# A graph layer with experts: the test for stray edges put off, the count matrix cleared by transfers, gathered chunks prepared first

## The chip, the cores and the metric

The kernel runs as one program on one core of a Trainium2 chip. The metric is the device time of one execution in microseconds (us); smaller is better. The kernel before has a median of 2081.84 us over three runs (2081.11 to 2084.28).

The engines have these names in the profile: PE (matrix products) with PEld (its loads of weights), DVE (elementwise work, reductions), ACT (elementwise work with functions), POOL (here: constants, clears, and the issue of indirect transfers) and SP (issues of plain transfers; its queue is SPq). ACT and POOL issue transfers too.

## The reference

There are 6,250 nodes with 256 features and 100,000 directed edges, sorted by destination. The destination of an edge is 6250 u^2 for a uniform u, so low nodes have many more edges than high ones; the sources are uniform.

```python
def _L0_gnn_ref(x, edge_index, weight, bias):
    src, dst = (edge_index[0], edge_index[1])
    summed = jax.ops.segment_sum(x[src], dst, num_segments=n)
    deg = jax.ops.segment_sum(ones, dst, num_segments=n)
    agg = summed / jnp.maximum(deg, 1.0)[:, None]
    out = jnp.concatenate([x, agg], axis=-1) @ weight
    return out / jnp.linalg.norm(out, axis=-1, keepdims=True) + bias
...
x = _layernorm(x + _L0_gnn_ref(x, edge_index, L0_gnn_weight, L0_gnn_bias), axis=-1)
...
deg_out = jnp.clip(jax.ops.segment_sum(ones, src, num_segments=n), 1.0)
deg_in = jnp.clip(jax.ops.segment_sum(ones, dst, num_segments=n), 1.0)
h = feats * jax.lax.rsqrt(deg_out)[:, None]
m = jax.ops.segment_sum(h[src], dst, num_segments=n) * jax.lax.rsqrt(deg_in)[:, None]
x = (m @ W_gc + b_gc) + (feats @ W_res + b_res)
y = x + _moe_ff(x, Wg, bg, w1, b1, w2, b2)   # top 2 of 64 experts
```

After that come a normalisation over the nodes, a residual and a second layer norm. The change concerns the two segment sums (each node's sum over the rows of its neighbours) and the degrees; the rest is the same in both kernels.

## The kernel before, in words

**Edges.** The edges are cut into 782 chunks of 128, in order of destination. For both layers the sums are made in two ways. The first 216 chunks hold all edges into the first 512 nodes and are *counted*: products of one-hot matrices on PE (L741, from selections that DVE builds at L727) give how often each source occurs for each destination, and DVE adds the counts into `adj`, a matrix of 49 x 816 bf16 on each of 128 partitions (L733). Later `adj` times the rows of all nodes is an ordinary dense product (L416). It has to be zero before the first count. The other 566 chunks are *gathered*: POOL issues one indirect transfer per chunk (L379, `gather_rows`), which brings the 128 source rows into `rows`, and a one-hot selection matrix `oh` sums them by destination on PE (L649 for rows of `x` in f32, L667 for rows in three bf16 parts). Neighbouring chunks make a group; the group's sum is turned (L386) and added into `acc` (L393), which is 2 x NACC f32 on each partition and has to be zero before that.

The first 64 of the gathered chunks take f32 rows of `x` itself, through seven buffers. The others take rows of `x3_rows`, three bf16 parts of `x`, which the kernel writes to DRAM first: SP loads five parts of `x` into `xt`, ACT casts them (L700), and SP writes `x3_rows`. They have nine buffers. For f32 rows `oh` is built by ACT for even chunks (L594 and L595, from `iota_row` and the column of `rel` for the chunk) and by DVE for odd ones (L592). The second layer gathers 518 chunks from `h_rows` in the same way (L1135).

**Preparation, L263 to L371.** ACT issues loads of the bias and of the weights `w0`. `nothing` is 512 zeros. `acc`'s first half is cleared by DVE (L266), the second half by ACT (L274); five eighths of `adj` by POOL (L270), the rest by ACT (L274). Then, on DVE in this order: the cast of `dst` to f32 (`dst_f`, L289); with `upmost` two products on PE that give the first destination of each chunk, copied to `first`; `base`, the first destination of a chunk's group, by a copy for each run of groups with the same size; `gbase`, the same by groups, and `base_i`, its integers; `wlo` and `whi`, the two halves of the window's node numbers; `rel`, an edge's destination less its base, for counted and for gathered chunks. Then the **test for stray edges**: an edge whose `rel` lies outside its window, or a group that lies before the dense part, sets `bad`; PE adds it over the partitions (`pbad`), and the result `any_bad` is 0 or 1. From it come `extra` (the trip counts 782 and 49, or 0), `sound` (1 or 0), and an offset OUTSIDE that is added to all of `rel`, so that with a stray edge no fast path counts anything. Then `hi` and `lo` of the sources, and `near`, the bf16 copy of `rel` for the gathered chunks.

**A way for any order.** Loops whose trip counts are read from `extra` (L437 in `any_order`, over all chunks, and L895 and L1202, over all 49 tiles of nodes) compute the layers edge by edge where the test has found a stray edge. With these inputs the trip counts are 0 and no body runs. The trip counts are loaded into registers at step 12 of the first stage (L878).

**Order.** In the first stage the order on PE, DVE, ACT and SP is written out by hand, and the engines' programs keep it: one step for each gathered chunk, and `work(i)` does what else is due at step i. A `Track` spreads its items evenly from step `begin` to step `end`: casts and writes of `x3_rows` until step 44 (X_END), counting until step 304 (A_END), the counts by source (`hist`, the out-degrees, through PSUM `ph`) until 350 (H_END), the dense product until 485 (D_END). `out_degrees` at H_END + 2 turns the counts by source into the factors of the second layer. The first layer's tiles follow as their nodes become complete (`first_layer`), with writes of `x1_rows` and `h_rows`. POOL is not part of this order: it issues the gathers one after the other, each as soon as its buffer is free.

The engines meet at the end of the first stage (the loops L437 and L895 with no trips, the first gather from `h_rows`) and at the end of the second stage (the loops of the second `any_order` and L1202). Then come the gating, the sorting of rows to the experts, and the experts.

Of the kernel before, what the change touches and what calls it, by code (L numbers as in the profile page):

```python
# [19 lines left out]
P = 128  # L20
# [125 lines left out]
def gnn_moe_kernel(  # L146
# [75 lines left out]
    sound = keep.tile([P, 1], F32, name="sound")  # L222

    with ExitStack() as gctx:
# [41 lines left out]
        nc.vector.memset(acc[:, 0, :], 0.0)  # L266
        flat = adj.rearrange("p t d -> p (t d)").bitcast(F32)
        total = NT * (DENSE + MORE) // 2
        by_pool = total * 5 // 8
        nc.gpsimd.memset(flat[:, :by_pool], 0.0)  # L270
        for v, a, b in ((acc[:, 1, :], 0, NACC), (flat, by_pool, total)):
            for i in range(a, b, 512):
                n = min(512, b - i)
                nc.scalar.copy(v[:, i : i + n], nothing[:, :n])  # L274
        with tc.tile_pool(name="pl", bufs=1) as pl, tc.tile_pool(name="pps", bufs=1, space=PSUM) as pps:
# [13 lines left out]
            nc.vector.tensor_copy(dst_f, dst_i)  # L289
            upmost = pl.tile([P, P], F32, name="upmost")  # L290
            nc.vector.tensor_scalar(upmost, ones, iota_p, None, op0=OP.is_gt)
            pfirst = pps.tile([P, 2, 512], F32, name="pfirst")
# [15 lines left out]
            for i, c0, col, g, n in runs:  # L308
                gv = first[:, c0 : c0 + n * g].rearrange("p (n g) -> p n g", g=g)
                nc.vector.tensor_copy(base[:, col : col + n * g].rearrange("p (n g) -> p n g", g=g),  # L310
                                      gv[:, :, 0:1].to_broadcast([P, n, g]))
# [3 lines left out]
            gbase = pl.tile([P, ng], F32, name="gbase")  # L315
            for i, c0, col, g, n in runs:
                nc.vector.tensor_copy(gbase[:, i : i + n],
                                      base[:, col : col + n * g].rearrange("p (n g) -> p g n", g=g)[:, 0, :])
            nc.vector.tensor_copy(base_i, gbase[0:1, :])
# [3 lines left out]
            wdst = pl.tile([P, ng], I32, name="wdst")  # L323
            nc.vector.tensor_scalar(wdst, gbase, iota_p, None, op0=OP.add)
            wtmp = pl.tile([P, ng], I32, name="wtmp")
            nc.vector.tensor_single_scalar(wtmp, wdst, 7, op=OP.arith_shift_right)
            nc.vector.tensor_copy(whi, wtmp)
            nc.vector.tensor_single_scalar(wtmp, wdst, P - 1, op=OP.bitwise_and)
            nc.vector.tensor_copy(wlo, wtmp)
            nc.vector.tensor_sub(rel[:, :DCH], dst_f[:, :DCH], base[:, :DCH])  # L330
            nc.vector.tensor_sub(rel[:, DCH:], dst_f[:, GCH:], base[:, DCH:])
# [13 lines left out]
            pbad = pps.tile([P, 2], F32, name="pbad")  # L345
            nc.tensor.matmul(pbad, ones, bad, start=True, stop=True)
            any_bad = pl.tile([P, 1], F32, name="any_bad")
            nc.vector.tensor_reduce(any_bad, pbad, AX.X, OP.max)
            nc.vector.tensor_scalar_min(any_bad, any_bad, 1.0)
            for k, n in enumerate((NCH, NT)):  # L350
                nc.vector.tensor_scalar(extra[:, k : k + 1], any_bad[0:1, :], float(n), None, op0=OP.mult)
            nc.vector.tensor_scalar(sound, any_bad, -1.0, 1.0, op0=OP.mult, op1=OP.add)
            nc.vector.tensor_scalar(any_bad, any_bad, OUTSIDE, None, op0=OP.mult)
# [11 lines left out]
            nc.vector.tensor_scalar(rel, rel, any_bad, None, op0=OP.add)  # L365
# [1274 lines left out]
```

## Time and profile before

| what | us or count |
|---|---|
| median of three runs | 2081.84 |
| the profiled execution, as timed | 2082.38 |
| its span, from the first to the last instruction | 2080.6 |
| PE busy | 1654.4 (80%) |
| DVE busy | 1104.8 (53%) |
| ACT busy | 693.4 (33%) |
| POOL busy | 1298.9 (62%) |
| mean granted clock of PE | 0.905 |
| transfers | 454.44 MB, mean 218 GB/s |
| gathers at L379 | 566 in the first stage, 518 in the second |
| mean duration of a gather's issue | 0.99 from `x` and `x3_rows` (x502 in the page's group, the others with the first rows), 0.96 from `h_rows` |

The span by stages, from the trace's stretches (start and end in us, what happens there, busy time of PE and POOL in it, mean GB/s):

| stretch | stage | PE | POOL | GB/s |
|---|---|---|---|---|
| 0 to 16 | constants, loads, clears | 0 | 15.35 | 91 |
| 16 to 107 | gathers from `x`, `x3_rows` written | 56.11 | 63.39 | 267 |
| 107 to 759 | gathers from `x3_rows`, counting, dense product | 509.09 | 498.34 | 228 |
| 759 to 791 | last tiles of the first layer, loops without trips | 8.92 | 2.13 | 85 |
| 791 to 1482 | gathers from `h_rows`, second dense product, second layer | 543.33 | 496.44 | 201 |
| 1482 to 2081 | gating, sorting, experts, normalisation | 536.98 | 223.24 | 232 |

The profile is one execution. Its lines give an engine's instruction with its line in the kernel, its duration, and the idle time ahead of it with the engine or transfer that ended that time. A busy share is a mean over stages that have different limits, so the waits and the timeline tell more than the shares: PE is busy for 80% of the span, but not at the same rate in all stages. POOL's busy time at L379 is the issue of the transfer, not the transfer itself.

### The profile page before, as it was taken

To read this page: it belongs to the slowest core of one execution; us is meant where nothing else is said; L and a number is where in the kernel's file an instruction comes from. 1 tells how busy PE (TensorE), PEld (TensorE's weight loads), DVE (VectorE), ACT (ScalarE), POOL (GpSimd) and SP (SyncE) were. 2 spreads that over 40 slices of the span, in tenths; PEclk is the share of its full clock that TensorE was granted. 3 is DMA by queue.
4 is the path that set the end of the run, shared out by engine and by line. 5 is a ranking of instruction groups with operands and counts; after the bars stand their busy time and mean duration, and the time that the engine had idled before them with its cause. 6 is when DMAs were issued, how large, how long until landed. Compare 5 with 4: busy or idle time off the path is not lost. (4 is left out here: it accounts for less than half of the span.)

```text
span 2080.6 us, 31816 instructions
## 1 busy us (share of the span) xinstructions
PE 1654.4 (80%) x8799; PEld 1183.2 (57%) x8861; DVE 1104.8 (53%) x3912; ACT 693.4 (33%) x1912; POOL 1298.9 (62%) x1490
## 2 busy tenths in 40 slices
PE   3777777768998656998777777777499998999697
PEld 1455555545666434665555554554278777878573
DVE  7656779954778862013445544454522333222497
ACT  5666666673333320001222222222122221222125
POOL 6777777777777746777777777776155554554100
PEclk9699999977999877999998998999599999999899
DMA  4966666667999856887777666665198997887343
GB/s 153 336 181 192 188 198 191 190 177 211 329 326 285 259 173 203 271 272 217 215 217 221 183 174 176 179 181 159 62 313 308 301 307 257 268 244 247 105 146 124
DMA packets 241291, 454.44 MB, mean 218 GB/s; under 512 B 36447, under 2 KB 159960, under 8 KB 241103
## 3 DMA queue, kind: packets, MB, share of 16 engines
q0 software_dynamic: 77952, 230.03, 37.8%
q1 hardware_dynamic: 160830, 220.73, 32.4%
q10 hardware_dynamic: 2320, 1.51, 0.3%
q8 instruction: 76, 1.25, 0.2%
q14 instruction: 113, 0.92, 0.1%
HBM read 386.44 MB, written 70.89 MB: 220 GB/s over the span
## 5 line engine op out<-in xcount | busy, mean ns | idle before, releaser
L379 POOL DMA_INDIRECT rows<-h_rows,src_i x518 | 496.9, 959 | 159.2 <-issue 75.3
L379 POOL DMA_INDIRECT rows<-x_rows,src_i x502 | 496.9, 990 | 153.0 <-issue 59.1
L667 PE MATMUL po<-rows,oh 128*128 128x256 bf16 (+1 forms) x1506 | 273.4, 297 | 111.5 <-DMA rows<-x_rows,src_i 104.7
L1135 PE MATMUL both_po<-rows,oh 128*128 128x256 bf16 x1554 | 248.2, 283 | 126.5 <-DMA rows<-h_rows,src_i 112.4
L1135 PEld LDWEIGHTS <-oh 128*128 128x128 bf16 x1554 | 172.3, 115 | 188.2 <-issue 149.8
L667 PEld LDWEIGHTS <-oh 128*128 128x128 bf16 x1506 | 163.3, 114 | 200.8 <-issue 144.9
L1403 POOL DMA_INDIRECT core<-ob,ix x100 | 101.5, 1015 | 196.0 <-DVE ob L1402 187.3
L1394 ACT ACTIVATE h<-ph,b1c 128x128 f32<-128x128 f32 (+1 forms) x288 | 94.3, 410 | 333.4 <-PE ph L1392 214.4
L1401 PE MATMUL po<-w2t,h 128*128 128x256 f32 x800 | 189.2, 385 | 1.0 <-ACT h L1394 0.5
L1401 PEld LDWEIGHTS po<-w2t,h 128*128 128x128 f32 x800 | 149.5, 191 | 38.6 <-ACT h L1394 18.9
L1402 DVE TENSOR_TENSOR ob<-po,b2b 128x256 f32<-128x256 f32 x100 | 42.4, 424 | 225.6 <-PE po L1401 214.9
L393 DVE TENSOR_TENSOR acc<-acc,pt 128x256 f32 x111 | 46.3, 417 | 209.1 <-PE pt L386 85.1
L594 ACT ACTIVATE oh<-iota_row,rel 128x128 bf16<-128x128 f32 (+1 forms) x280 | 110.8, 396 | 65.0 <-PE po L667 40.0
L401 DVE TENSOR_TENSOR oh<-iota_lo,near 128x512 bf16<-128x512 bf16 x194 | 78.9, 417 | 82.0 <-PE both_po L1135 80.9
L1380 PE MATMUL ph<-xt,w1t 128*128 128x256 f32 x448 | 118.6, 405 | 0.0
L741 PE MATMUL pa<-oha,ohl 128*128 128x490 bf16 x264 | 100.3, 386 | 22.4 <-DVE adj L733 21.6
L416 PE MATMUL pd<-adj,x 128*128 128x304 bf16 (+1 forms) x569 | 115.5, 336 | 2.1 <-DMA x<-h_rows 0.9
L1360 POOL DMA_INDIRECT xb<-xx_tok,ix x100 | 99.1, 991 | 26.8 <-issue 25.5
L595 ACT ACTIVATE oh<-oh,ones 128x128 bf16<-128x128 bf16 (+1 forms) x280 | 112.5, 402 | 9.1
L727 DVE TENSOR_SCALAR oha<-iota_h,rel 128x490 bf16<-128x490 f16 x264 | 95.2, 368 | 35.7 <-PE pa L741 35.1
L1380 PEld LDWEIGHTS ph<-xt,w1t 128*128 128x128 f32 x448 | 110.4, 326 | 5.4 <-issue 2.6
L733 DVE TENSOR_TENSOR adj<-adj,pa 128x490 f32 x146 | 98.0, 671 | 22.7 <-PE pa L741 18.9
(322 smaller groups left out, 3078.5 us busy)
## 6 DMA issues: line engine op xcount, KB each, us to landing
w1t<-in_L_gnn_w_dram SPq DMA_DIRECT2D x72, 512.0 KB
w2t<-in_L_gnn_w_dram SPq DMA_DIRECT2D x72, 512.0 KB
core<-zero SPq DMA_DIRECT2D x7, 1792.0 KB
ys<-core SPq DMA_DIRECT2D x48, 256.0 KB
x3d<-x_rows SPq DMA_DIRECT2D x49, 192.0 KB
h_rows<-h SPq DMA_DIRECT2D x49, 192.0 KB
x<-h_rows SPq DMA_DIRECT2D x49, 192.0 KB
x_rows<-x SPq DMA_DIRECT2D x24, 384.0 KB
```

Source lines behind the costliest of these rows:

```text
L379: nc.gpsimd.indirect_dma_start(out=r, out_offset=None, in_=table, in_offset=bass.IndirectOffsetOnAxis(ap=index, axis=0))
L416: nc.tensor.matmul(pd[h, w], side(x3, s, h), adj[:, t, a:b], start=(t == 0 and s == 0), stop=(t == NT - 1 and s == 2))
L594: nc.scalar.activation(oh, iota_row, AF.Abs, bias=r, scale=-1.0)
L595: nc.scalar.activation(oh, oh, AF.Relu, bias=ones[:, 0:1], scale=-1.0)
L667: nc.tensor.matmul(po[:, :w], oh, r[:, s * D : s * D + w], start=(ch == c0 and s == 2), stop=(ch == c0 + g - 1 and s == 2))
L733: nc.vector.tensor_add(a, a, pa)
L741: nc.tensor.matmul(pa[0].rearrange("p t w -> p (t w)"), lows[ch - ch % OHB][:, :, ch % OHB], places.pop(ch), start=first, stop=last)
L1135: nc.tensor.matmul(po, oh, r[:, :, s, :], start=(ch == c0 and s == 0), stop=(ch == c0 + g - 1 and s == 2))
L1360: nc.gpsimd.indirect_dma_start(out=xb[:, h, :], out_offset=None, in_=xx_tok, in_offset=bass.IndirectOffsetOnAxis(ap=ix[:, 0, h : h + 1], a ...
L1380: nc.tensor.matmul(ph[:, hc], w1m[:, c, hc, :], xt[:, c], start=(c == 0), stop=(c == 1))
L1401: nc.tensor.matmul(po, h1[:, hc, h, :], w2t[:, hc * D : (hc + 1) * D], start=(hc == 0), stop=(hc == 3))
L1403: i = nc.gpsimd.indirect_dma_start(out=core, out_offset=bass.IndirectOffsetOnAxis(ap=ix[:, 1, h : h + 1], axis=0), in_=ob[:, h, :], in_off ...
```

## The change

1. The clear of `adj` goes from POOL and ACT to four transfers inside SBUF, issued by ACT: three of 13 x 512 f32 on each partition, and one of what is left over (24 f32 on each partition), all read from `nothing`. Both halves of `acc` are cleared by ACT, by 26 copies.
2. The preparation is put into another order: `upmost` ahead of the cast of `dst`; bases, `rel`, group bases, `wlo` and `whi`, and `near` for the gathered chunks first, then the same for the counted ones.
3. The test no longer ends in the preparation. It leaves `doubt`, one value per partition. `out_degrees`, at step H_END + 2, tests `hist` as well (a count by source of 256 or more), takes the maximum with `doubt`, adds over the partitions on PE (`pf`, in a pool of PSUM of its own) and makes `extra` and `sound` there. `rel` is not moved by OUTSIDE any more; the sums that the fast path has made are cleared instead, by a new function `clear_sums`, a loop over the tiles of `acc` whose trip count is 0 where no stray edge was found. It stands ahead of both `any_order` calls. `deg` and `hist` are multiplied by `sound`.
4. The trip counts are loaded at step H_END + 40 instead of step 12.
5. Of the f32 chunks, odd ones up to chunk 12 of the gathered ones have their `oh` built by ACT; DVE builds the odd ones after that.

```diff
-        nc.vector.memset(acc[:, 0, :], 0.0)
         flat = adj.rearrange("p t d -> p (t d)").bitcast(F32)
         total = NT * (DENSE + MORE) // 2
-        by_pool = total * 5 // 8
-        nc.gpsimd.memset(flat[:, :by_pool], 0.0)
-        for v, a, b in ((acc[:, 1, :], 0, NACC), (flat, by_pool, total)):
-            for i in range(a, b, 512):
-                n = min(512, b - i)
-                nc.scalar.copy(v[:, i : i + n], nothing[:, :n])
+        for i in range(0, total, 13 * 512):
+            r = min(13, (total - i) // 512)
+            if not r:
+                break
+            nc.scalar.dma_start(flat[:, i : i + r * 512].rearrange("p (r c) -> p r c", c=512),
+                                nothing[:, None, :].to_broadcast([P, r, 512]))
+        if total % 512:
+            nc.scalar.dma_start(flat[:, total - total % 512 :], nothing[:, : total % 512])
+        for h in range(2):
+            for i in range(0, NACC, 512):
+                n = min(512, NACC - i)
+                nc.scalar.copy(acc[:, h, i : i + n], nothing[:, :n])
...
-            nc.vector.tensor_copy(dst_f, dst_i)
             upmost = pl.tile([P, P], F32, name="upmost")
             nc.vector.tensor_scalar(upmost, ones, iota_p, None, op0=OP.is_gt)
+            nc.vector.tensor_copy(dst_f, dst_i)
...
+            bases(of_gathered)
+            nc.vector.tensor_sub(rel[:, DCH:], dst_f[:, GCH:], base[:, DCH:])
+            group_bases(of_gathered)
+            wdst = pl.tile([P, ng], I32, name="wdst")
+            wtmp = pl.tile([P, ng], I32, name="wtmp")
+
+            wins = slice(len(DGRP), ng)
+            nc.vector.tensor_copy(base_i[:, wins], gbase[0:1, wins])
+            nc.vector.tensor_scalar(wdst[:, wins], gbase[:, wins], iota_p, None, op0=OP.add)
+            nc.vector.tensor_single_scalar(wtmp[:, wins], wdst[:, wins], 7, op=OP.arith_shift_right)
+            nc.vector.tensor_copy(whi[:, wins], wtmp[:, wins])
+            nc.vector.tensor_single_scalar(wtmp[:, wins], wdst[:, wins], P - 1, op=OP.bitwise_and)
+            nc.vector.tensor_copy(wlo[:, wins], wtmp[:, wins])
+
+            nc.vector.memset(near[:, NG:], OUTSIDE)
+            nc.vector.tensor_copy(near[:, :NG], rel[:, DCH:])
+
+            bases(of_counted)
...
+            group_bases(of_counted)
+            nc.vector.tensor_copy(base_i[:, : len(DGRP)], gbase[0:1, : len(DGRP)])
...
-            pbad = pps.tile([P, 2], F32, name="pbad")
-            nc.tensor.matmul(pbad, ones, bad, start=True, stop=True)
-            any_bad = pl.tile([P, 1], F32, name="any_bad")
-            nc.vector.tensor_reduce(any_bad, pbad, AX.X, OP.max)
-            nc.vector.tensor_scalar_min(any_bad, any_bad, 1.0)
-            for k, n in enumerate((NCH, NT)):
-                nc.vector.tensor_scalar(extra[:, k : k + 1], any_bad[0:1, :], float(n), None, op0=OP.mult)
-            nc.vector.tensor_scalar(sound, any_bad, -1.0, 1.0, op0=OP.mult, op1=OP.add)
-            nc.vector.tensor_scalar(any_bad, any_bad, OUTSIDE, None, op0=OP.mult)
+            nc.vector.tensor_reduce(doubt, bad, AX.X, OP.max)
...
-            nc.vector.tensor_scalar(rel, rel, any_bad, None, op0=OP.add)
-
-            nc.vector.memset(near[:, NG:], OUTSIDE)
-            nc.vector.tensor_copy(near[:, :NG], rel[:, DCH:])
...
+        def clear_sums():
+
+            with tc.For_i(0, trips[1], 1) as t:
+                one = ones[:, None, :].to_broadcast([P, 2, P])
+                nc.vector.tensor_sub(acc[:, :, ds(t * P, P)], one, one)
...
-                if dt == F32 and ch % 2:
+                if dt == F32 and ch % 2 and ch - GCH > 12:
...
-            def out_degrees(ph):
-                nc.vector.tensor_add(hist, hist, ph)
+            def out_degrees(ph, psf):
+
+
+                over = wk.tile([P, 2], F32, name="over", bufs=1)
+                nc.vector.tensor_reduce(over[:, 0:1], hist, AX.X, OP.max)
+                nc.vector.tensor_scalar(over[:, 0:1], over[:, 0:1], 256.0, None, op0=OP.is_ge)
+                nc.vector.tensor_max(over[:, 1:2], over[:, 0:1], doubt)
+                pf = psf.tile([P, 1], F32, name="pf")
+                nc.tensor.matmul(pf, ones, over[:, 1:2], start=True, stop=True)
+                nc.vector.tensor_scalar_min(doubt, pf, 1.0)
+                for k, n in enumerate((NCH, NT)):
+                    nc.vector.tensor_scalar(extra[:, k : k + 1], doubt[0:1, :], float(n), None, op0=OP.mult)
+                nc.vector.tensor_scalar(sound, doubt, -1.0, 1.0, op0=OP.mult, op1=OP.add)
+                nc.vector.scalar_tensor_tensor(hist, hist, sound, ph, op0=OP.mult, op1=OP.add)
...
-                        out_degrees(ph)
+                        with tc.tile_pool(name="psf", bufs=1, space=PSUM) as psf:
+                            out_degrees(ph, psf)
...
-                    if i == 12:
+                    if i == H_END + 40:
                         for k, n in enumerate((NCH, NT)):
                             trips.append(nc.values_load(extra[0:1, k : k + 1], min_val=0, max_val=n))
...
+        clear_sums()
+        nc.vector.tensor_scalar(deg, deg, sound, None, op0=OP.mult)
         any_order(x, True)
...
+        clear_sums()
         any_order(h3_rows, False)
```

`bases` and `group_bases` are the two copy loops of before, each over a part of the runs (`of_gathered`, `of_counted`); `wins` is the part of the group columns that belongs to gathered groups.

More of the change, by code (lines that the diff above doesn't have):

```diff
@@ L222, in gnn_moe_kernel @@
     sound = keep.tile([P, 1], F32, name="sound")
+    doubt = keep.tile([P, 1], F32, name="doubt")
     with ExitStack() as gctx:
@@ L307, in gnn_moe_kernel, with bases, group_bases @@
                     runs.append([i, c0, col, g, 1])
[L308 to L311, printed above, removed]
+            gbase = pl.tile([P, ng], F32, name="gbase")
+            of_gathered = [r for r in runs if r[0] >= len(DGRP)]
+            of_counted = [r for r in runs if r[0] < len(DGRP)]
+            def bases(some):
+                for i, c0, col, g, n in some:
+                    gv = first[:, c0 : c0 + n * g].rearrange("p (n g) -> p n g", g=g)
+                    nc.vector.tensor_copy(base[:, col : col + n * g].rearrange("p (n g) -> p n g", g=g),
+                                          gv[:, :, 0:1].to_broadcast([P, n, g]))
+            def group_bases(some):
+                for i, c0, col, g, n in some:
+                    nc.vector.tensor_copy(gbase[:, i : i + n],
+                                          base[:, col : col + n * g].rearrange("p (n g) -> p g n", g=g)[:, 0, :])
+            bases(of_gathered)
[13 more added lines that the diff above has]
+            bases(of_counted)
             nc.vector.tensor_scalar_min(base[:, :GCH], base[:, :GCH], float(DENSE - DWIN))
@@ L314, in gnn_moe_kernel @@
                                     op0=OP.max, op1=OP.min)
[L315 to L319, printed above, removed]
+            group_bases(of_counted)
+            nc.vector.tensor_copy(base_i[:, : len(DGRP)], gbase[0:1, : len(DGRP)])
             more = slice(len(edge_groups(0, GCH, DWIN, DMAXG)), len(DGRP))
             nc.vector.tensor_scalar(base_i[:, more], gbase[0:1, more], float(DENSE - EDGE), None, op0=OP.add)
[L323 to L329, printed above, removed]
             nc.vector.tensor_sub(rel[:, :DCH], dst_f[:, :DCH], base[:, :DCH])
-            nc.vector.tensor_sub(rel[:, DCH:], dst_f[:, GCH:], base[:, DCH:])
             out_w = pl.tile([P, WREL], F32, name="out_w")
```

## The prediction

> **What bounds the kernel now.** I read the list of waits of the Pool engine first, then the timeline of the first 60 us, then the stretches of DMA traffic, and last the timeline around the two zero-trip loops at the end of the first gather stage. In the waits each line gives the waiting tile and line, who released it, the total in us, the count and the longest.
>
> ```profile
> POOL rows L379 <- issue: 144.4, 474, 0.3
> ...
> POOL rows L379 <- PE po L649: 14.4, 18, 9.2
> ```
>
> Nearly all idle time before the 1,084 gathers of L379 is the 0.3 us between two issues. Only three waits are longer: these 9.2 us near the start, 1.7 us in the second stage (for PE at L416), and the change of stage (29.8 us, for the last write of `h_rows`). So Pool's stream of gathers sets the pace from the first gather to the end of the second gather stage, and whatever moves its start moves the end by as much. This is the start (start, duration, engine, line, operation; in brackets the idle time before it and who ended it):
>
> ```profile
> 3.91 10.50 POOL L270 MEMSET adj<- 128x12495 f32 x1
> 8.43 7.94 DVE L289 CAST dst_f<-dst_i 128x782 f32<-128x782 int32 x1
> ...
> 14.36 1.59 POOL L285 MEMSET need<- 128x1 f32 x46
> 16.13 1.23 POOL L379 DMA_INDIRECT rows<-in_x_dram,src_i  x1 [0.18 <-issue]
> ...
> 31.70 0.40 ACT L594 ACTIVATE oh<-iota_row,rel 128x128 f32<-128x128 f32 x1 [14.41 <-DVE rel L365]
> ...
> 32.59 5.19 PE L649 MATMUL po<-rows,oh 128*128 128x257 f32 x14 [2.55 <-ACT oh L595]
> ...
> 34.09 0.95 POOL L379 DMA_INDIRECT rows<-in_x_dram,src_i  x1 [9.19 <-PE po L649]
> ```
>
> Pool clears `adj`, issues the seven gathers that there are buffers for, and then stands for 9.19 us until PE has used the first buffer. PE waits for the selection matrix `oh` of chunk 0, which ACT builds from `rel`, which DVE finishes at 31.60. The eighth gather, at 34.09, is the clock of all that follows. Its distance to PE's start is 34.09 - 32.59 = 1.50 us, and PE's to ACT's 32.59 - 31.70 = 0.89 us.
>
> **The change, part by part.**
>
> *Pool.* Without L270 (10.50 us) the need memsets end at 3.91 + 1.59 = 5.5 and the first seven gathers run from about 5.7 to 5.7 + 7 x 1.25 = 14.4. This alone brings nothing: the eighth waits for PE as before.
>
> *DVE.* Gone from its front are the `acc` memset (5.39) and most of the 7.94 us of L289, which ends with Pool's memsets at 16.4 while the casts behind it take 0.6. `dst_i` has landed by about 8. Cast 0.7, the two products on PE 2.98, the copy 0.97, twelve base copies at 0.1, the subtraction 0.73: `rel` of the gathered chunks stands at about 16. The test's tail (30.08 to 31.60) falls away. The later half of the preparation (about 10 us of rows of L310 to L371) ends near 26 and holds the `xt` loads on SP until then, against 31.76 before. So DVE would free PE some 15 us earlier.
>
> *ACT is what comes late instead.* In the built kernel ACT issues three clears of 13 x 2 KB on each partition and a small fourth one, then loads its table, then clears both halves of `acc`, then builds `oh` for chunk 0. The fourth clear reuses the landing semaphore of the first and stands in ACT's queue until the first has landed. All of ACT is queued behind it: 26 copies, the `oh` of chunks 0 to 12 (the odd ones too, now), so PE, so Pool's eighth gather. When does the first clear land? It moves 128 x 13 x 2,048 B = 3.41 MB. The stretches show what the DMA engines carry (share busy and GB/s are the last two columns):
>
> ```profile
> 5.00:6.00 1.00, 0.00 (x0) 0.00 (x0) 1.00 (x1) 1.00 (x3) 1.00 (x1) 1.00 1.03 374
> ...
> 1074.00:1076.00 2.00, 0.00 (x0) 0.00 (x0) 0.00 (x0) 0.00 (x0) 1.50 (x2) 0.52 1.06 388
> ```
>
> The last row is a bulk transfer out of SBUF (`core<-zero`) beside gathers: 388 GB/s with the engines full. By 5 us 0.47 MB of the 1.46 MB of first loads have moved (117, 169 and 174 GB/s in the three us before). The rest, 0.99 MB, the clear's 3.41 and the seven gathers' 0.92 MB are 5.32 MB, at 390 GB/s 13.6 us: landed at 18.6 to 19; I take 18.8. Bounds: 16.3 if no gather gets between; 20.5 if the first loads end at 8.6 as now and every gather delays it. From there: the small issue 0.4, table load 1.28 (now at 1.71, hidden), 26 copies at 6.64 / 13 = 0.51, so 13.3, then 0.89 to PE and 1.50 to Pool: 17.4. The eighth gather is issued at 18.8 + 17.4 = 36.2, **2.1 us later** than 34.09 (bounds -0.4 and +3.8).
>
> That such a wait holds the whole engine is read from the trace's nearest case, ACT idle for 2.45 us on a landing (784.11 below); if it did not, the sum would be the first rival's. The Trainium skill, "DMA: Bandwidth & Descriptors", section "Anatomy of one DMA — SWDGE (gpsimd) path", has a rule against this change: a DMA engine never waits for a semaphore, the issuing sequencer does so before it dispatches. "SBUF — State Buffer", section "Summary: rules for kernel authors", gives 436 GB/s for SBUF to SBUF alone: by it the first clear alone would take 7.8 us instead of 8.7, an estimate, and the sum be about 1 us less; no run here shows such a transfer.
>
> *The rest of the clear.* All of it is 10.24 MB, 26 us of full engines, ending near 40 us. Behind it stand the `xt` loads (five of 256 KB), needed only when ACT reaches its first cast, at about 40. SP's first and third write of `x3` wait for the second and third clear (near 28 and 38 at the same rate) and are due after 41. The engines are full from 40 to 100 us in both kernels. The last `x3` write is issued at 98.6 and the next load that waits for those lanes at 100.76, while Pool's first gather of `x3` rows comes at 106.59: 5.8 us of cover, of which I count 3 used up. If the cover goes, what exceeds it is paid in full.
>
> *Six odd `oh` moved from DVE to ACT*: 0.73 us each (ACT starts them at 31.70, 32.44, 33.17), below Pool's 1.25 per gather, which hides them; without it 4.4.
>
> *Test at step H_END + 2.* Seven more small DVE rows (0.13 to 0.19 each, 1.0 us) and one trip to PE and back (29.45 to 30.08, 0.6). PE waits meanwhile, with the chunks behind it; nine buffers at 1.28 us hide it. Without that cover 1.6 us. The register loads move from 42.9 to step 390, where the same buffers hide them. The scaling of `deg` is one row of 0.2, in front of DVE work that waits anyhow.
>
> *Two more loops with no trips.* At its exit each engine waits for all work and all transfers issued before it. The nearest rows:
>
> ```profile
> 774.88 0.42 ACT L523 ACTIVATE junk<-o 128x256 f32<-128x256 f32 x1
> ...
> 781.52 6.09 SPq L556 DMA_DIRECT2D h_rows<-h  x2
> ...
> 784.11 0.40 ACT L551 CAST h<-rv 128x256 bf16<-128x256 f32 x1 [2.45 <-DMA h_rows<-h]
> ```
>
> At today's loop a write issued at 781.52 lets ACT go on at 784.11, 2.6 us later. The new loop stands, in the built kernel, right after SP's write of `x1_rows` that is now issued at 774.32: exit at about 776.9 + 0.3, where ACT now goes on at 774.88: **2.3 us**. In the second stage the work before it ends with PE at 1464.88 and no transfer is pending; ACT leaves today's last loop there 0.35 us and PE 1.0 us after the last work: **0.7 us**. Bounds for each: 0 (waits cannot gain) and the 4.55 us that DVE stood still at today's loop, whose body on DVE is long (its next row is at 786.73).
>
> Sum: 2.1 + 2.3 + 0.7 = +5.1 us on the profiled span of 2080.6, so 2085.7. That execution was timed at 2082.38 and the median is 2081.84; 5.1 on the median is 2086.9.
>
> **The rivals.** *First, the other side: ACT is not held.* If the fourth clear's wait costs nothing, ACT is through its copies at 2.6 + 0.4 + 1.28 + 13.3 = 17.6, the eighth gather goes out at 20.0 instead of 34.09, -14.1, and with 3.0 for the loops -11.1: 2070.7. For it: Pool and DVE are indeed ready by 16. Against: the first clear would have to land by 3 us; it decides as soon as it lands before 9.5, where front and loops together pass -4.2. Chance 0.08.
>
> *Second, the sums cancel.* The clear lands at 14 to 16.5 because the queue of the clear gets more than its turn, or the loops are half hidden: front -2 to 0, loops +2 to +3, in all about +1.2, 2083.0. For it: the gathers' share of the engines is my guess. Chance 0.26.
>
> *Third, SBUF to SBUF runs at half the rate.* No row shows such a transfer. The first clear takes 17.5 us, lands near 28, front +11; the clear lasts 52 us and the `x3` writes end some 26 us late against 5.8 of cover and the shift of 11, so about +20 in front, with the loops +23: 2105. Chance 0.12.
>
> **How the numbers follow.** Forecast 0.54, with its own range +2.6 to +9 (2084.4 to 2090.8); the rivals have 0.46. The time is the forecast's 2086.9. The range leaves out the first rival and the heart of the third, and takes in the upper bounds of front and loops (3.8 + 9.1): 2081 to 2095. A measurement of this kernel tells about 0.2%, 4.2 us, from no change. Slower: the third rival and some 0.48 of the forecast, 0.60; within: 0.06 of the forecast and the second rival, 0.32; faster: 0.08.
>
> **What would show it.** ACT's first `acc` copy near 20 and not near 4; its first `oh` near 33.5, with PE right behind; Pool's seven gathers from 5.7 to 14.4 and then a wait of some 20 us instead of 9; the eighth gather at 36.2; no wait of Pool at its first `x3` gather; the change of stage 2.3 us longer than 30.6 from gather to gather. An eighth gather before 30, or one after 40, makes the forecast wrong; so does a Pool wait at the first `x3` gather.

## The result: 15 us slower, and the profile after

The changed kernel has a median of 2098.03 us over four runs (2095.08 to 2099.51) against 2082.81 for the kernel before (2081.11 to 2084.28); the ratio is 1.0072, with an interval from 1.0054 to 1.0089. It is slower, as forecast, but by 15.2 us where 5.1 were forecast, and it lies outside the range of 2081 to 2095.

The waits of the Pool engine in the changed kernel (who waited, for whom; total in us, times, longest) show where to look:

```profile
POOL rows L391 <- issue: 151.1, 496, 0.3
...
POOL rows L391 <- PE po L667: 35.8, 19, 30.4
POOL iota_b L1014 <- DMA h_rows<-h: 31.7, 1, 31.7
```

The 9.2 us near the start have become 30.4, and the wait at the change of stage, 29.8, has become 31.7. Nothing else above 1.4 us stands before a gather of the two stages. This is the start of the changed kernel (timeline: start, duration, engine, line, operation; ACTq is ACT's queue of transfer issues):

```profile
1.73 17.62 ACTq L273 DMA_DIRECT2D adj<-nothing  x3
...
14.84 0.94 POOL L391 DMA_INDIRECT rows<-in_x_dram,src_i  x1 [0.30 <-issue]
15.03 0.73 DVE L331 TENSOR_TENSOR rel<-dst_f,base 128x566 f32<-128x566 f32 x1
...
19.40 9.96 ACTq L276 DMA_DIRECT2D adj<-nothing  x1
...
29.39 1.28 ACT L280 ACT_TABLE_LOAD   x1 [29.39 <-issue]
30.68 13.17 ACT L280 COPY acc<-nothing 128x512 f32<-128x512 f32 x26
43.76 0.40 ACT L612 ACTIVATE oh<-iota_row,rel 128x128 f32<-128x128 f32 x1
...
44.64 5.57 PE L667 MATMUL po<-rows,oh 128*128 128x257 f32 x15 [32.03 <-ACT oh L613]
...
46.14 0.94 POOL L391 DMA_INDIRECT rows<-in_x_dram,src_i  x1 [30.36 <-PE po L667]
```

Pool has issued its seven gathers by 15.8 and DVE has `rel` ready at 15.8. Everything waits for ACT. ACT's three large clears take 17.6 us to *issue*, and the small fourth one, 96 bytes on each partition, another 9.96. Only at 29.4 does ACT load its table. From there the distances are those of the working: 13.17 of copies, 0.88 to PE, 1.50 to Pool. The eighth gather goes out at 46.14, 12.05 us later than before.

Its delay can be followed from gather to gather: the 64th is 12.07 late (121.17 against 109.10), the last of the first stage 11.4, the first from `h_rows` 13.4 (803.99 against 790.57), the last of all 14.0, and the first gather of the expert stage 14.85 (1515.82 against 1500.97). The rest of the 16.8 us between the two spans lies in the stretch of the experts, 452.0 us long after and 449.6 before; that stretch varies by itself, as the controls below show. So the front makes 12, the two stage ends about 3.

### The profile page after: what moved, and what is told of

It reads as the page before. It is cut to its first block, busy times and chain, and to the rows that moved or that the text cites. A ratio compares the mean times of both kernels' runs of the same rounds, so it can differ in the third digit from the quotient of the medians.

```text
span 2097.4 us, 31979 instructions
## 1 busy us (share of the span) xinstructions
PE 1646.8 (79%) x8799; PEld 1176.6 (56%) x8861; DVE 1089.7 (52%) x3908; ACT 696.9 (33%) x1922; POOL 1287.1 (61%) x1489
## 5 line engine op out<-in xcount | busy, mean ns | idle before, releaser
L685 PE MATMUL po<-rows,oh 128*128 128x256 bf16 (+1 forms) x1506 | 267.2, 292 | 114.3 <-DMA rows<-x_rows,src_i 105.4
L1394 POOL DMA_INDIRECT xb<-xx_tok,ix x100 | 98.5, 985 | 26.9 <-issue 25.6
```

The costliest lines, as they stand in the source:

```text
L685: nc.tensor.matmul(po[:, :w], oh, r[:, s * D : s * D + w], start=(ch == c0 and s == 2), stop=(ch == c0 + g - 1 and s == 2))
L1394: nc.gpsimd.indirect_dma_start(out=xb[:, h, :], out_offset=None, in_=xx_tok, in_offset=bass.IndirectOffsetOnAxis(ap=ix[:, 0, h : h + 1], a ...
```

## The experiments

All times are compared with the kernel before, run on the same chip. On most of these chips the kernel before takes what it took in the result. Four kernels (the one without the loops, the wide source, two controls) ran on another chip, where the kernel before takes 2301 us; of these only the front of the trace and distances on that same chip are read. The ratio is estimated over all runs and can differ a little from the quotient of the two medians.

| kernel | median us | kernel before | ratio (interval) | eighth gather at |
|---|---|---|---|---|
| before | 2082.81 | | | 34.09 |
| changed | 2098.03 | 2082.81 | 1.0072 (1.0054 to 1.0089) | 46.14 |
| small clear on DVE | 2088.02 | 2082.35 | 1.0024 (1.0011 to 1.0037) | 36.45 |
| small clear first | 2087.98 | 2082.35 | 1.0024 (1.0011 to 1.0036) | 36.20 |
| clears in 13 pieces | 2101.44 (one run) | 2081.95 | | 49.01 |
| clears issued by SP | 2085.72 | 2082.35 | 1.0016 (1.0004 to 1.0028) | 18.98 |
| old clears | 2081.07 | 2082.35 | 0.9988 (0.9975 to 1.0002) | 26.10 |
| `adj` cleared in steps | 2078.32 | 2081.95 | 0.9985 (0.9974 to 0.9996) | 19.74 |
| the same, one loop | 2075.24 | 2081.95 | 0.9971 (0.9959 to 0.9983) | 19.60 |
| no loops, other chip | 2314.94 | 2301.37 | 1.0067 (1.0046 to 1.0089) | 46.55 |
| wide source, other chip | 2312.47 | 2301.37 | 1.0042 (1.0023 to 1.0061) | 18.40 |

### What holds ACT: the small clear taken away, or put first

Two explanations fit the trace. Either an issue returns only when the queue has taken the transfers ahead of it (the *backlog*), or it waits for a *landing semaphore*, the counter that a transfer raises when it has landed and that a later transfer uses again.

```diff
-            nc.scalar.dma_start(flat[:, total - total % 512 :], nothing[:, : total % 512])
+            nc.vector.memset(flat[:, total - total % 512 :], 0.0)
```

> The changed kernel with the last 24 columns of adj cleared by a DVE memset instead of a fourth transfer; nothing is left out. Backlog theory (an issue on ACT's queue returns only when the transfer ahead of it has all its packets in the queue, and about 90 packets per DMA engine fit): the last issue is now the third, which returned at 19.36 us, so the copies start at about 20.7 and the eighth gather goes out at 46.14 - 9.96 = 36.2 instead of 46.14; time about 2088. Rival, landing semaphores (the fourth issue stood for the landing of an earlier clear): the same, 2088. Rival, ACT's hold does not set the gather: the eighth gather stays near 46, time 2098.

The second kernel issues the same small transfer ahead of the three large ones.

> The changed kernel with the small transfer issued ahead of the three large ones, so that no clear reuses the landing semaphore of another clear; nothing is left out. Backlog theory: the third large clear is the last issue and returns when the second is in the queue, at about 19.5 us; eighth gather at 36.2, time about 2088, as with the small clear on DVE. Rival, landing semaphores: no wait for a clear is left, ACT goes on by about 9 us (the landing of dst_i, whose semaphore the last one reuses), eighth gather at about 26, time about 2078. Rival, a small transfer costs 10 us wherever it stands: eighth gather near 46, time 2098.

The timeline of ACT with the small clear on DVE, and then Pool's:

```profile
1.70 17.96 ACTq L273 DMA_DIRECT2D adj<-nothing  x3
19.69 1.28 ACT L280 ACT_TABLE_LOAD   x1 [19.69 <-DVE base L349]
...
36.45 0.94 POOL L391 DMA_INDIRECT rows<-in_x_dram,src_i  x1 [20.11 <-PE po L667]
```

and with the small clear first:

```profile
1.72 0.55 ACTq L270 DMA_DIRECT2D adj<-nothing  x1
2.30 17.11 ACTq L275 DMA_DIRECT2D adj<-nothing  x3
19.44 1.28 ACT L280 ACT_TABLE_LOAD   x1 [19.44 <-DVE base L349]
```

Both give back 10 us and land on 2088. The small transfer costs 0.55 us when it is first, so it isn't slow by itself. In the second kernel none of the clears reuses the landing semaphore of another, yet ACT is held until 19.4 all the same; the rival of the semaphores had it free by 9. What holds ACT is the issue itself, and how long depends on what stands ahead of it on the queue: only an issue behind a large transfer is held.

### How much a queue takes: pieces, and wide rows

The transfer records of the trace tell how many packets of the clears had started when an issue returned. In the changed kernel a large clear is 1,664 packets of 2 KB, 104 for each of the 16 DMA engines:

```
issue that returns     at us   packets ahead of it   started   still queued, per engine
changed, 2nd clear      8.98          1664              217            90
changed, 3rd clear     19.36          3328             1905            89
changed, 4th (small)   29.36          4992             3680            82
small first, last      19.41          3328             1899            89
```

"Ahead of it" counts the transfers issued before, not the one that returns. An issue returns when the transfers before it are down to some 82 to 90 packets per engine. The next kernel cuts the same clear into 13 transfers of 24 packets per engine (steps of `3 * 512` for `13 * 512` in the loop, and the small clear on DVE).

> The changed kernel with the clear of adj by transfers cut into 13 pieces of 3 x 512 columns on ACT's queue and the last 24 columns cleared by DVE; nothing is left out. The pieces are 24 packets per DMA engine each, 312 in all. Backlog theory by packets (an issue returns when the transfer ahead of it is in a queue that holds about 90 packets per engine): the last issue returns when 288 - 90 = 198 packets per engine have gone, which the changed kernel reached at about 26 us; copies start at 27.3, the eighth gather at about 43. Rival, two transfers at a time (an issue returns when the transfer two ahead of it has landed): the last issue returns when 264 packets per engine have gone, at about 33.4 us, and the eighth gather goes out at about 50. Rival, it was the small transfer or the order of large ones: ACT is held until 19.5 as with three pieces, eighth gather near 36.

None of the three expectations is met as a whole: the last issue returned at 32.2 and the eighth gather went out at 49.01, near what two transfers at a time would give, but not for that reason. The issues one by one (ACT's queue) tell why:

```profile
11.21 4.59 ACTq L273 DMA_DIRECT2D adj<-nothing  x1
15.84 2.50 ACTq L273 DMA_DIRECT2D adj<-nothing  x1
22.83 0.60 ACTq L273 DMA_DIRECT2D adj<-nothing  x1
26.56 0.60 ACTq L273 DMA_DIRECT2D adj<-nothing  x1
```

These are the eighth to eleventh pieces. The eighth returns at 15.80 and the ninth at 18.34, with 81 and 82 packets per engine queued ahead of each; the sixth piece, two ahead of the eighth, landed only at 22.35, so "two transfers at a time" is refuted. The fourth to seventh returned at 94, 93, 90 and 103 (with the packets of the weights, which lie ahead of them on the same queue). From the tenth on it is another wait: its issue takes only 0.60, but starts at 22.83, 0.5 us after that landing, whose semaphore it reuses in the built kernel. So both waits exist. With 13 pieces the semaphores set when the last four go; with 3 + 1 the backlog sets the time.

The backlog of an engine's own queue is not all that lengthens an issue. SP's five loads of `xt` have at most 64 packets per engine ahead of them on SP's queue, and still take 6.41 us to issue in the changed kernel, while ACT's clears are queued; in a kernel without clears by transfer (the one below that clears in steps) they take 2.44, as in the kernel before:

```profile
23.27 6.41 SPq L698 DMA_DIRECT2D xt<-in_x_dram  x5
```

```profile
24.76 2.44 SPq L690 DMA_DIRECT2D xt<-in_x_dram  x5
```

What makes them slower isn't shown. Each of SP's issues takes at most 1.6 us here, ACT's held ones 6.5 to 10.3.

Is the backlog counted in packets or in bytes? The next kernel reads zeros from a wide source, so that one row is one packet of 25.6 KB (these lines stand in place of the loop and the small clear; ACT copies the second half of `acc`):

```diff
+        nc.vector.memset(acc[:, 0, :], 0.0)
+        for i in range(0, 3 * NACC, NACC):
+            nc.scalar.dma_start(flat[:, i : i + NACC], acc[:, 0, :])
+        nc.vector.memset(flat[:, 3 * NACC :], 0.0)
```

> The changed kernel with the clear of adj by three transfers whose source is the first half of acc, cleared by DVE first, so that a row of a transfer is 25.6 KB in one piece instead of 13 pieces of 2 KB (the 792 columns left over by DVE, the second half of acc by ACT); nothing is left out. If the queue's backlog is counted in packets and the rows stay whole, no issue is held (24 packets per DMA engine in all): the third returns about 1.5 us after the first starts (about 8 to 9 us), and the eighth gather goes out near 20. If it is counted in bytes (90 packets of 2 KB are 180 KB per engine), the third returns near 20 as before, and the eighth gather goes out near 24.5. If the rows are cut to 2 KB packets, the same as by bytes. In each case xt lands behind the clears, near 40, ACT stands at its first cast as with SP's clears, and the time is that of that kernel, 2085.7, give or take 2.

The timeline of ACT and Pool, and PE's of the same kernel:

```profile
8.40 3.16 ACTq L271 DMA_DIRECT2D adj<-acc  x3
...
18.40 1.55 POOL L386 DMA_INDIRECT rows<-in_x_dram,src_i  x1 [1.67 <-PE po L662]
```

```profile
21.67 1.20 PE L662 MATMUL po<-rows,oh 128*128 128x257 f32 x2 [3.54 <-DMA rows<-in_x_dram,src_i]
24.63 1.20 PE L662 MATMUL po<-rows,oh 128*128 128x257 f32 x2 [1.77 <-DMA rows<-in_x_dram,src_i]
28.97 1.20 PE L662 MATMUL po<-rows,oh 128*128 128x257 f32 x2 [3.15 <-DMA rows<-in_x_dram,src_i]
```

Nearly the same bytes (9.83 MB for 10.22) are issued in 3.16 us, so packets count, not bytes. When the third issue returns, 14 packets per engine are still queued ahead of it, 358 KB; the clears of 2 KB packets held ACT until 168 to 184 KB were left. The records show 384 packets of 25,600 bytes, most of which take 1.2 to 1.5 us of a DMA engine. There is a new price that I had not expected: the rows of a gather queue among these packets, and PE waits 1.7 to 3.6 us for each chunk's rows until the clear ends near 45 us. This is the other chip, so the total (1.0042) isn't compared with that of kernels on the first ones; what was expected of it, the time of SP's clears, can't be judged.

### Clears issued by SP: the hold gone, the transfers still in the way

The four clears go behind the load of `dst_i`, as `nc.sync.dma_start`.

> The changed kernel with all four clears issued by SP, right behind its load of dst_i, instead of by ACT; nothing is left out. Backlog theory: SP stands until about 29.5 us, and ACT is free at once: table and copies end near 16, rel of the gathered chunks stands at 15.8, so oh at 16.7, PE at 17.6, the eighth gather near 19.5 (26.6 earlier than in the changed kernel). The xt loads go out at 29.5 instead of 23.3 and land behind the clears, near 42; the writes of x3_rows run some 56 us from then, to about 99, while Pool wants its first row of x3_rows at 19.5 + 75 = 94.5: a new wait of 4 to 8 us there. Net 2098 - 26.6 + 6 = 2077. Rival, the transfers are too slow for an early start: the wait at x3_rows takes back nearly all, 2090 or more. Rival, ACT's hold was not what set the gather: 2098.

The front came as expected, 18.98. The rest did not, and the place of the new wait wasn't the one that I named (timeline of SP, ACT, Pool):

```profile
30.39 8.40 SPq L698 DMA_DIRECT2D xt<-in_x_dram  x5
41.35 0.62 ACT L700 CAST x<-xt 128x512 bf16<-128x512 f32 x1 [18.11 <-DMA xt<-in_x_dram]
...
44.26 1.22 POOL L391 DMA_INDIRECT rows<-in_x_dram,src_i  x1 [13.70 <-PE po L667]
```

The `xt` loads leave SP only at 30.4 and land behind the clears at 41. ACT, in the order written by hand, stands at its first cast of `xt` for 18 us with the next `oh` behind it, and Pool for 13.7. By the 64th gather 1.9 us of the 15.1 are left (107.25 against 109.10). With the loops that is +1, and the median says +3.4 (interval +0.8 to +5.8).

### The rest of the change by itself

`adj` and `acc` are cleared as in the kernel before (Pool, DVE, ACT); the new order, the late test and the loops stay.

> The changed kernel with adj and acc cleared as before (Pool, DVE, ACT), so that only the new order of the preparation, the late test and the loops remain of the change; nothing is left out. My theory, that the clears alone cost time and the new order gains: the cast of dst still ends with Pool's memset near 16.4, rel about 7 us behind it, the eighth gather near 26 instead of 34.09 (-8), the loops +2.8, and up to 2 us of wait at the first row of x3_rows: 2076 to 2080. Rival, the new order brings nothing: eighth gather near 34 and 2085 with the loops. Rival, something else of the change is slow: 2090 or more.

The eighth gather goes out at 26.10, 8.0 earlier than before, as worked out: the new order does bring `rel` forward. (The cast still ends with Pool's memset, at 16.4.) The sum expected was -5 us; the medians differ by 1.3, the ratio stands for 2.5 (interval -5.2 to +0.4), so a gain isn't shown, nor is the sum refuted. The trace of this run is 7.8 us ahead at the first gather of the expert stage, and loses 5.8 in that stage, which took 455.4 us.

Then `adj` without any transfer, cleared by DVE in small pieces in the steps of the first stage, where it is not needed before step 53:

```diff
+                    if 0 < i <= X_END and (i - 1) * 512 < total:
+                        nc.vector.memset(flat[:, (i - 1) * 512 : min(i * 512, total)], 0.0)
```

> The changed kernel with no transfers for adj: DVE clears it by 40 memsets of 512 columns, one at each of steps 1 to 40, ahead of the first count at step 53; nothing is left out. If what costs the time is the clear by transfers (ACT held by the queue, then xt behind the clears), then ACT's copies end at 16, the eighth gather goes out near 19.5 as with SP's clears, and no wait follows at the first cast, as the xt loads land at about 26. The eighth gather is 14.6 earlier than in the kernel before, the loops give back 2.9: 2082.3 - 11.7 = 2070.6, if the later stages keep their length. Rival, the stage of f32 chunks is bound by its transfers (24 MB at 390 GB/s are 63 us): then the wait comes back at the first row of x3_rows and the gain is 4 to 8, 2074 to 2078. Rival, a later stage sets the end, whatever the front does: 2081 or more.

> The same as the kernel that clears adj in steps, and the new loop of clear_sums is put into one outer loop with the loop over the chunks (trip count 0 or 1), so that there is one loop without trips in each place where there were two; nothing is left out. My theory (each loop without trips makes the engines meet once): 2.1 us gained at the end of the first stage and 0.8 at the end of the second, 2.9 less than its sister. Rival, the loops cost nothing that the median shows: equal.

The eighth gather goes out at 19.74 and 19.60, ACT stands at its first cast for 4.5 us only, which Pool does not feel, and there is no wait at the first row of `x3_rows`. The stage of f32 chunks gives back 3.6 us up to the 64th gather (78.6 and 78.5 us from the eighth against 75.0). In the first of the two 1.1 of it is one wait of 1.38 us for PE; the rest, and all of it in the second, is that Pool's issues of gathers take longer (60.5 and 61.5 us in this stage against 57.9), for a reason that isn't shown. So 10.8 and 11.0 are left there. The medians gain 3.6 and 6.7, less than the 11.7 and 14.6 expected; the first is closer to the rival's 4 to 8, but without the wait at the first row of `x3_rows` that the rival had for it. The one-loop version is the fastest of all, faster than the kernel before by 0.29% (0.17 to 0.41).

### The loops, and the stretch of the experts

> The changed kernel without its two calls of clear_sums (left out: the clearing of acc where a stray edge is found, which never happens with these inputs). Each loop without trips makes the engines meet once: by the profile of the changed kernel 2.0 us at the end of the first gather stage (32.6 from gather to gather against 30.6) and 0.8 at the end of the second, so 2098.0 - 2.8 = 2095.2. Rival, the loops are hidden by what they stand beside: 2098. The eighth gather stays at 46.1.

On the other chip the distance from the last gather of the first stage to the first from `h_rows` is 30.5 us without the loops; two kernels with them on that chip have 32.8 and 31.6, and the kernel before has 29.7. The changed kernel on the first chip has 32.6, the kernel before 30.6. The ratio of 1.0067 is not far from the changed kernel's 1.0072, but the chips differ. The pair of kernels in steps gives a price for both places: 2078.32 with two loops in each place, 2075.24 with one, 3.1 us, where 2.9 was expected; as the runs of each kernel spread over 8 to 9 us, this is good to some 2 us.

For the second place the traces are clear. This is ACT's row right behind that place in the changed kernel, in the kernel before and in the one-loop kernel:

```profile
1479.60 0.53 ACT L1066 ACTIVATE xl<-pG,rsq_in 128x320 f32<-128x320 f32 x1 [0.99 <-PE pG L1062]
```

```profile
1464.92 0.53 ACT L1033 ACTIVATE xl<-pG,rsq_in 128x320 f32<-128x320 f32 x1 [0.23 <-PE pG L1029]
```

```profile
1457.99 0.53 ACT L1061 ACTIVATE xl<-pG,rsq_in 128x320 f32<-128x320 f32 x1 [0.23 <-PE pG L1057]
```

The wait is 0.23 in every profile without the second loop (the kernel before three times, no loops, one loop) and 0.69 to 0.99 in all others. At the first place ACT waits 1.5 to 1.9 us for a write of `x1_rows` in every profile with the new loop, and this wait is gone without loops and with one. But with one loop the first gather from `h_rows` still comes 32.7 us after the last of the first stage, against 33.3 with two, so something else fills part of it. By these distances the loop's price there lies anywhere from 0.6 us (this pair) over 2.0 (the changed kernel and the kernel before) to 2.3 (the other chip), and isn't settled.

> The kernel before once more, for the stretch of the experts (first gather of that stage to the first load of ys): 449.6 and 454.1 us in its two profiles so far, 452.0 to 455.8 in the eight of other kernels. If it varies by itself, 449 to 456 again; if the changed kernels lengthen it, 449 to 451.

> The kernel with the old clears and the rest of the change once more, for the same stretch: its median gained 1.3 us where its eighth gather is 8.0 earlier and its loops give back 2.9, so some 4 us are missing, and its profile shows 455.4 us for the stretch of the experts. If that is chance, 449 to 456 at random; if it belongs to the kernel, 454 to 456 again. Eighth gather at 26.1.

The other control is the kernel before, profiled again on the chip of the kernels in pieces and in steps:

> The kernel before, unchanged, profiled a second time, to see how far the stretches of one execution vary: the distance from the last gather of the second stage to the first gather of the expert stage (55.4 us before), and from there to the first load of ys (449.6 before; 452 to 456 in the five profiles of changed kernels). If the stretch of the experts is 449 to 451 again, the changed kernels lengthen it, by 2 to 5 us, which none of my terms holds. If it is 453 or more, it varies by itself. Eighth gather at 34.1 either way.

From the first gather of the experts to the first load of `ys` the kernel before took 449.6, 454.1 and 452.6 us in its three profiles, other kernels 452.0 to 457.4 in eleven; the old clears had 455.4 and 455.0. So 454 us belong to the unchanged kernel too, and a single span can be 5 us off for this alone. The means, 452.1 and 454.4, differ by less than that spread. Against the profile of the kernel before on their own chip (454.1) the two kernels in steps lose nothing in this stretch (454.5 and 453.0). Whether an earlier start makes this stretch longer stays open.

On the other chip the same kernel runs in another way. These are rows of stretches for the kernel before, on the first chip and on that one (busy time of PE, PEld, DVE, ACT, POOL; granted clock of PE, DMA share, GB/s):

```profile
110.00:860.00 750.00, 577.73 (x3761) 409.19 (x3786) 512.86 (x1682) 353.85 (x1004) 550.62 (x560) 0.89 0.75 224
```

```profile
110.00:860.00 750.00, 544.29 (x3349) 371.44 (x3350) 487.70 (x1587) 337.96 (x968) 496.44 (x502) 0.84 0.67 197
```

On the first chip this stretch takes in the end of the first stage and 69 us of the second; on the other one all of it lies in the first stage, so the counts (3,761 and 3,349 products of PE) are not of the same work. Within the first stage gathers follow each other every 1.50 us there and every 1.29 on the first chip, and before 92 of its gathers Pool waits for PE (L667 and L741), 0.9 us on average. PE's own products are only 2 to 7% longer there (304 ns against 297 at L667, 415 against 387 at L741), and PE stands still in waits for which the profile names no cause, these above all:

```profile
PE pa L741 <- issue: 36.2, 39, 3.6
```

Between 110 and 750 us such waits of PE come to 71.6 us, on the first chip to 0.2. So Pool waits for PE on that chip, but the lower granted clock (0.84 for 0.89) doesn't account for it alone, and the cause isn't shown.

## Why the prediction was right or wrong, point by point

- *Pool's stream of gathers carries any shift of its start.* Right on the chip of the result: 12.05 us late at the eighth gather, 12.07 at the 64th. On the other chip, where Pool waits for PE, only part arrives: the kernel without the loops is 12.45 late at the eighth gather and 11.0 at the last of the first stage, the old clears are 8.3 early and 4.5.
- *Pool and DVE are ready by 16, ACT comes late.* Right: 15.8 for both, though Pool's first gather went out at 6.88, not 5.7, as it waited for the load of `src_i`. The preparation ended at 23.1, not 26.
- *The first clear lands at 18.8.* Right: 18.6 by the transfer records. The share of the engines that I guessed for it was good enough; SBUF to SBUF runs at the rate that was counted with (84 ns for a packet of 2 KB on each of 16 engines, 390 GB/s), so the third rival is out. All clears had landed by 39.4, where 40 was worked out.
- *"From there: the small issue 0.4."* **This is the step that failed.** The small issue took 9.96 us. I took an issue as 0.4 us plus a wait for a semaphore, and all of ACT's hold for that one wait. The runs show that an issue returns only when the transfers ahead of it on its queue are down to 82 to 90 packets per DMA engine (81 to 103 with pieces), and without any wait for a semaphore: with the small clear first no semaphore of a clear is used again, and ACT is held all the same. The second and third large clears were held in the same way, for 6.5 and 10.3 us, and ended near the landing that I had counted with by coincidence: when the last of the large ones returned, at 19.36, the first had just landed. The small one then waited for the third to enter the queue. The working had the right engine and the right start; the term is off by 9.6, and 2.1 + 9.6 = 11.7 of the measured 12.05.
- *Table, copies, PE, Pool: 1.28 + 13.3 + 0.89 + 1.50.* Measured 1.28, 13.17, 0.88, 1.50.
- *Cover at the first row of `x3_rows`.* Right: the last write was issued at 109.8, the first gather of these rows at 118.67, without a wait.
- *Six `oh` on ACT, the test at H_END + 2, the later load of the trip counts: hidden.* Right; no gather of the first stage behind the eighth waited more than 0.31 us.
- *The loops: 2.3 and 0.7.* Measured 2.0 from gather to gather at the first place (32.6 against 30.6; the kernel before has 31.1 in its second profile on a 2082 us chip, so this is good to some 0.5), and 0.76 at the second (ACT's wait of 0.99 against 0.23). In the changed kernel the new loop is seen where ACT and DVE, between two tiles, wait for a write of `x1_rows`, and the old one where they did before:

```profile
787.87 0.42 ACT L541 ACTIVATE junk<-o 128x256 f32<-128x256 f32 x1 [1.87 <-DMA x_rows<-o]
...
797.31 0.40 ACT L569 CAST h<-rv 128x256 bf16<-128x256 f32 x1 [2.37 <-DMA h_rows<-h]
```

- *The sum.* 12.05 + 2.0 + 0.8 = 14.9 for 5.1; the median says 15.2. The range took its upper bound for the front, 3.8, from the time of the landing alone, and so missed a wait that comes after it.
- *The rivals.* The first (ACT not held) needed the clear to be free of ACT's queue; the kernel with SP's clears makes this true and is still not faster, since the `xt` loads then land behind the clears. That was priced nowhere in the rival. The second and third did not come.

What stays open: the kernels with an earlier front gain less in the median than their gathers show (1.3, or 2.5 by the ratio, for some 5 us; 3.6 for some 8). The profile of the old clears loses it in the stretch of the experts; chance and cause aren't told apart.

## What to carry to other kernels

An engine that issues transfers is held at the issue, without any semaphore, as soon as the transfers ahead on its queue have more packets left than the queue takes (81 to 103 per DMA engine here). Before moving a clear or copy to an engine's queue, count its packets per DMA engine, and ask what the engine has to do next; put large issues on an engine that is idle, last in line, or not at all. And look whose loads will land behind those bytes: taking away ACT's hold only moved the wait to the loads of `xt`, while clearing in small pieces where the result isn't due for 50 steps cost at most 3.6 us of the 14 gained in front.

## What the runs showed of the hardware that was not expected

- ACT's queue took 81 to 103 packets per DMA engine before the next issue was held, with packets of 2 KB; three transfers of 25.6 KB packets, 24 per engine in all, went in within 3.2 us. The count is of packets. SP was held in the same way when it issued the clears (10.4 us for the small one).
- Most packets of 25.6 KB took 1.2 to 1.5 us on a DMA engine, and gathers that share the engines with them landed late: PE waited 1.7 to 3.6 us for each chunk.
- Issues on SP's queue, with at most 64 packets per engine ahead of them there, took up to 1.6 us while ACT's clears were queued, and 0.47 without them; the cause is open.
- The same kernel took 2082 us on some chips and 2301 on another. Between 110 and 860 us the granted clock was 0.89 against 0.84, and PE stood still for 71.6 us without a cause in the profile against 0.2 (110 to 750); why isn't shown.
